# A graph layer and a mixture of experts on one core: a tile's work as stages at fixed chunk offsets, two first-layer blocks to a bank, nine short steps first

## The chip, the cores and the metric

The kernel runs on one core of a Trainium2 chip. Its time is the device time of one execution in microseconds (us), and the kernel before took 1339.35 us, the median of 11 runs (1335.19 to 1341.65).

The engines are named as in the profile: PE (TensorE, the matmuls), PEld (its loads of weights, which overlap with the matmuls), DVE (VectorE), ACT (ScalarE), POOL (GpSimd) and SP (SyncE). Each engine executes its own instructions in the order in which the program has them, and waits for the others by semaphores. SPq, ACTq and POOLq are the queues from which an engine starts DMA transfers.

## The reference

6250 nodes have 256 features each. The first layer is a graph convolution over 106250 edges, sorted by target. The second routes every node to the best two of eight experts, each of which is a feed-forward net of 256 to 1024 to 256.

```python
deg_isqrt = jnp.maximum(segment_sum(ones, dst), 1.0) ** (-0.5)
x = x + gnn(layernorm(x))        # norm * segment_sum((norm * (h @ W.T + b))[src], dst)
h = layernorm(x)
scores = h @ Wg.T + bg           # 8 experts
top, idx = top_k(scores, 2); p = softmax(top)
out = sum over the two e of p_e * (relu(h @ W1[e].T + b1[e]) @ W2[e].T + b2[e])
x = x + out
```

Everything is float32.

## The kernel before, in words

The nodes are 49 tiles of 128. After an opening stage (degrees, and a table of the scaled inputs in DRAM) the kernel has a **stream** and a **tail**.

**The stream** is a loop over 831 chunks of 128 edges; an iteration is called a slot here. In each slot `gather` has POOL start an indirect DMA that fetches 128 rows of the table (6 chunks ahead, 24 buffers), `mask` has DVE make the 128x128 matrix that says which edge goes to which node, and `add_up` has PE add the chunk to a sum in PSUM (`ps`). Once all chunks of a tile are in, the tile goes through `join` (DVE sums, ACT copies to `whole`), `turn_sum` (PE transposes, ACT copies), `linear` (PE, tile `pt`) and `route`: DVE normalizes, scores and chooses two experts, PE counts places (`pt` again), and `sort` and `send` order the tile's rows by expert and write them to eight queues in DRAM (`fhq`), 8 DMAs on SP.

**A step** of the experts takes up to 256 rows (four short steps at the end: 128) from the fullest queue. `choose` decides on DVE which; `fetch` has SP load the expert's weights and biases `w1` (1.15 MB) and `w2` (1.03 MB) and the rows `xT`. `up` is one of the 8 blocks of the first layer: PE multiplies into a PSUM tile `ph`, ACT applies bias and relu and writes `hid`. `down` is a quarter of the second layer's work for 128 rows (PSUM tile `py`), after the last of which DVE adds the bias (`y`) and SP writes the result to DRAM (`fyq`). A step of 256 rows is 16 such pieces, 8 of `up` and 8 of `down`; a step of 128 is 8 and 4. `next_piece` puts one piece into the program in each slot of the stream, and a second one in every fourth slot while the next step is ready.

PSUM has eight banks of 2 KB per partition. `ph` has two buffers, each a tile of its own of 256 columns.

**The tail** goes on after the last chunk: one piece per slot, the loads of the remaining steps, and the way back. `read_back` has POOL fetch each node's two results from `fyq` by indirect DMAs (98 in all), DVE adds them to the node's row (`xr`), and the rows are stored. The list `DONE` says after which step which tiles may be read back.

The order in which everything stands in each engine's program is written out by hand: `plan_at` puts a call into a slot, and `in_parts` spreads a generator over slots in a row (one part per slot). In the kernel before, `route` and `fetch` are such generators. 56 steps are planned: 49 that follow tiles 3 to 48 (three tiles are followed by two), then 7.

These lines are the ones that the change of PSUM tiles touches:

```python
ph = psp.tile([P, FT], F32, name="ph")
for k in range(2):
    nc.tensor.matmul(ph[:, :n], w1[...], f["xT"][:, :n, k], start=(k == 0), stop=(k == 1))
nc.scalar.activation(f["hid"][:, b, :n], ph[:, :n], AF.Relu, bias=w1[...])
```

Of the kernel before, what the change touches and what calls it, by code (L numbers as in the profile page):

```python
# [28 lines left out]
NE = 8  # L29
# [8 lines left out]
FIRST_STEP = 3  # L38
EXTRA = (42, 44, 46)
FOLLOWS = [t for t in range(FIRST_STEP, NT) for _ in range(1 + (t in EXTRA))]  # L40
USUAL = len(FOLLOWS) + 7
SHORT = 4
# [16 lines left out]
DONE = ((40, 29), (42, 33), (43, 34), (44, 35), (45, 36), (46, 38), (47, 39), (48, 40), (49, 41), (50, 42),  # L59
        (51, 44), (52, 45), (53, 46), (54, 47), (USUAL - 1, NT))  # L60
LATER = 1 << 17

# [39 lines left out]
LATE = [(3 if FINAL[t + 1] - FINAL[t] == 9 else 2) if t < NT - 2 else 0 for t in range(NT)]  # L102
# [30 lines left out]
def in_order(ctx: ExitStack, tc: tile.TileContext, g: Shared):  # L133
# [8 lines left out]
    yq = dram.tile([P + USUAL * FT, D], F32, name="fyq")  # L142
# [208 lines left out]
    for step, t1 in DONE:  # L351
        nc.vector.memset(bounds[:, t0:t1, :], float(P + (step + 1) * FT))
        t0 = t1
# [21 lines left out]
    zero = keep.tile([P, FT * D // P], F32, name="zero")  # L375
    nc.gpsimd.memset(zero, 0.0)  # L376

# [15 lines left out]
    def mask(c):  # L393
        masks[c] = work.tile([P, P], F16, name="mask", bufs=MASKS + 3)
        r = (P - BASE[c] % P) % P
        nc.vector.tensor_scalar(masks[c], g.col_b[:, r:r + P], g.rel[:, c:c + 1], None, op0=OP.is_equal)  # L396
# [53 lines left out]
    def clear_results():  # L450

        for step in range(USUAL - SHORT, USUAL):
            r0 = P + step * FT + P
            nc.sync.dma_start(yq[r0:r0 + FT - P, :], zero[:, :D])

# [7 lines left out]
    whole, turned_sums, turned_inputs = {}, {}, {}  # L465
# [4 lines left out]
    def join(w):  # L470
# [11 lines left out]
        rolled = new  # L482
        for t, p0, p1 in pieces(n0, n1):
            if p0 == 0:
                whole[t] = work.tile([P, D], F32, name="whole")
            nc.scalar.activation(whole[t][p0:p1, :], new[p0:p1, :], AF.Copy)  # L486

    def turn_sum(t):
        pt = psp.tile([P, 2, P], F32, name="pt", bufs=1)
        u = whole.pop(t)  # L490
        for k in range(2):
            nc.tensor.transpose(pt[:, k, :], u[:, k * P:(k + 1) * P], g.ident)
        uT = work.tile([P, 2, P], F32, name="uT")
        nc.scalar.activation(uT, pt, AF.Copy)
        turned_sums[t] = uT
# [8 lines left out]
    def route(t):  # L504

        nonlocal placed, known, sent
        xt = g.xr[:, t, :]
        pl = turned_sums.pop(t)
        nc.vector.scalar_tensor_tensor(xt, pl[:, :D], g.norm[:, t:t + 1], xt, op0=OP.mult, op1=OP.add)  # L509
        score = work.tile([P, NE], F32, name="score")  # L510
        nc.vector.scalar_tensor_tensor(score, pl[:, D:], g.norm[:, t:t + 1], xg[:, t, :], op0=OP.mult, op1=OP.add)
        yield
        st = work.tile([P, 6], F32, name="st")
        nc.vector.bn_stats(st, xt)
        mv = work.tile([P, 2], F32, name="mv")
        nc.vector.bn_aggr(mv, st)
        v = work.tile([P, 1], F32, name="v")
        nc.vector.tensor_scalar(v, mv[:, 1:2], EPS, None, op0=OP.add)
        yield

# [4 lines left out]
        rstd = guess.bitcast(F32)  # L525
        vh = work.tile([P, 1], F32, name="rv")
        nc.vector.tensor_scalar(vh, v, -0.5, None, op0=OP.mult)
        r = work.tile([P, 1], F32, name="rs")
        for i in range(3):
            if i == 1:  # L530
                yield
            nc.vector.tensor_scalar(r, rstd, rstd, vh, op0=OP.mult, op1=OP.mult)
            nc.vector.tensor_scalar(rstd, r, 1.5, rstd, op0=OP.add, op1=OP.mult)
        yield

        nc.vector.scalar_tensor_tensor(score, minus, mv[:, 0:1], score, op0=OP.mult, op1=OP.add)
        sc = work.tile([P, NE], F32, name="sc")
        nc.vector.scalar_tensor_tensor(sc, score, rstd, bgs, op0=OP.mult, op1=OP.add)
        times = work.tile([P, 1], F32, name="times")
        nc.vector.tensor_scalar(times, rstd, UP, None, op0=OP.mult)  # L540

        mx = work.tile([P, NE], F32, name="mx")
        nc.vector.max(mx, sc)
        ix = work.tile([P, NE], U32, name="ix")
        nc.vector.max_index(ix, mx, sc)
        ixf = work.tile([P, 2], F32, name="ixf")
        nc.vector.tensor_copy(ixf, ix[:, 0:2])
        yield
        sel = work.tile([P, 2, NE], F32, name="sel")
        for j in range(2):  # L550
            nc.vector.tensor_scalar(sel[:, j], g.col_f[:, :NE], ixf[:, j:j + 1], None, op0=OP.is_equal)
        if t == NT - 1:
            nc.vector.tensor_scalar(sel, sel, valid, None, op0=OP.mult)
        chose = work.tile([P, 2, NE], BF16, name="chose")
        both, front = chose[:, 0], chose[:, 1]
        nc.vector.tensor_add(both, sel[:, 0], sel[:, 1])

        nc.vector.tensor_scalar(front, g.col_f[:, :NE], ixf[:, 0:1], None, op0=OP.is_gt)
        nc.vector.scalar_tensor_tensor(front, g.col_f[:, :NE], ixf[:, 1:2], front, op0=OP.is_gt, op1=OP.add)
        if t == NT - 1:  # L560
            nc.vector.tensor_scalar(front, front, valid, None, op0=OP.mult)
        ex = work.tile([P, 1], F32, name="ex")
        nc.vector.tensor_sub(ex, mx[:, 1:2], mx[:, 0:1])
        nc.scalar.activation(ex, ex, AF.Exp)
        yield

        for _ in range(LATE[t]):
            yield
        h2 = work.tile([P, D], F32, name="h2", bufs=3)
        nc.vector.tensor_scalar(h2, xt, mv[:, 0:1], times, op0=OP.subtract, op1=OP.mult)  # L570
        h2s[t] = work.tile([P, 2, D], F16, name="h2s", bufs=3)
        nc.scalar.activation(h2s[t][:, 0], h2, AF.Copy)
        yield
        pp = psp.tile([P, 3, NE], F32, name="pt", bufs=1)
        nc.tensor.matmul(pp[:, 0], below, chose[:, 0], start=True, stop=True)
        nc.tensor.matmul(pp[:, 1:3], every, chose, start=True, stop=True)
        nc.vector.tensor_sub(h2s[t][:, 1], h2, h2s[t][:, 0])
        pr = prob[:, t, :]
        nc.vector.tensor_scalar(pr[:, 1:2], ex, 1.0, None, op0=OP.add)
        nc.vector.reciprocal(pr[:, 0:1], pr[:, 1:2])  # L580
        nc.vector.tensor_mul(pr[:, 1:2], ex, pr[:, 0:1])
        col = work.tile([1, 2, NE], I32, name="col")
        nc.vector.tensor_sub(col[:, 0], filled[0:1, :], head[0:1, :])
        columns_of[t] = col
        yield

        totals = work.tile([P, 2, NE], F32, name="totals")
        nc.vector.tensor_copy(totals, pp[:, 1:3])
        place = work.tile([P, NE], F32, name="place")
        nc.vector.tensor_add(place, pp[:, 0], filled)  # L590
        nc.vector.tensor_add(filled, totals[:, 0], filled)
        nc.vector.tensor_max(most, totals[:, 0], most)
        placed += 1
        spot = work.tile([P, NE], F32, name="spot")
        nc.vector.tensor_add(spot, pp[:, 0], totals[:, 1])  # L595
# [863 lines left out]
```

## Time and profile before

| | |
|---|---|
| runs (11) | 1339.35 us median, 1335.19 to 1341.65 |
| the profiled execution: own time, span | 1338.88 us, 1337.1 us |
| PE busy (share of the span) | 1178.9 us (88%) |
| PEld | 899.4 us (67%) |
| DVE | 985.5 us (74%) |
| POOL | 903.5 us (68%) |
| ACT | 402.4 us (30%) |
| first gather, last gather (start) | 82.33 us, 1127.41 us |
| last chunk added up (start) | 1145.43 us |
| last group of second-layer matmuls (start) | 1315.65 us |

The profile is one execution. Its span runs from the first instruction to the last; the execution's own time is 1.8 us longer than the span, and 0.5 us shorter than the median of the runs. Busy times of PE overstate it, since matmuls are pipelined and their ends are modelled. Matmuls in float32 stand twice in the trace for each one in the program: a step's 16 for the first layer are 32 rows.

### The profile page before, as it was taken

The numbers are of one execution on the slowest core, as the hardware profiler recorded it, in microseconds if no ns is written. First come the engines' busy times: TensorE is split into PE (matmuls) and PEld (weight loads), VectorE is DVE, ScalarE is ACT, GpSimd is POOL, SyncE is SP. The second block draws the span as 40 slices with busy tenths as digits, with TensorE's granted clock in tenths as the row PEclk, the third lists the DMA queues.
The fourth block names the chain that finished last, engine by engine and source line by source line (L and its number), as shares of the span: only waits on it lengthen the run. The fifth ranks groups of instructions, "written<-read, shape, count | busy, mean of one in ns | idle before, by whom it ended". The sixth has DMA issues, their size and how long they took to land.

```text
span 1337.1 us, 23956 instructions
## 1 busy us (share of the span) xinstructions
PE 1178.9 (88%) x6224; PEld 899.4 (67%) x6224; DVE 985.5 (74%) x5327; ACT 402.4 (30%) x931; POOL 903.5 (68%) x984
## 2 busy tenths in 40 slices
PE   4529895999899999999999989999999999799984
PEld 4417663776677677776766766777777777678873
DVE  8842658787888888888788887788877775765542
ACT  2622331232323233233332323232232322222221
POOL 2047777777777777777777777777777775347742
PEclk9999777999999999999999998999999999899987
DMA  8343446888687887877778787878878987679882
GB/s 298 112 158 106 121 137 196 266 253 286 211 287 227 287 261 253 286 241 270 250 261 268 245 279 218 274 243 288 286 234 286 296 295 254 235 244 347 305 304 89
DMA packets 158459, 326.16 MB, mean 244 GB/s; under 512 B 26708, under 2 KB 105256, under 8 KB 143976
## 3 DMA queue, kind: packets, MB, share of 16 engines
q1 hardware_dynamic: 110780, 194.17, 41.5%
q0 software_dynamic: 46864, 129.82, 32.3%
q8 instruction: 51, 0.84, 0.3%
q14 instruction: 96, 0.79, 0.2%
q10 hardware_dynamic: 668, 0.55, 0.1%
HBM read 269.01 MB, written 55.42 MB: 243 GB/s over the span
## 4 chain that ended last, share of the span: by engine, by line
PE 56%; DMA 17%; DVE 15%; issue 4%; ACT 3%; SPq 2%; POOL 2%; POOLq 0%; ACTq 0%; DVEq 0%
PE ph L730 22%; PE py L740 16%; PE ps L403 9%; DMA rows<-ftable,src 7%; DMA xT<-fhq 5%; PE pt L501 3%; DMA fhq<-ordered 2%; PE ph L446 2%; SPq L641 2%; DMA yb<-fyq,rowat 2%; DVE mask L396 2%; PE px L629 2%; PE px L435 1%; DVE rolled L481 1%; DVE y L744 1%
## 5 line engine op out<-in xcount | busy, mean ns | idle before, releaser
L389 POOL DMA_INDIRECT rows<-ftable,src x831 | 791.2, 952 | 253.4 <-issue 99.5
L730 PE MATMUL ph<-xT,w 128*128 128x256 f32 (+1 forms) x1792 | 468.3, 390 | 28.8 <-DMA xT<-fhq 19.0
L740 PE MATMUL py<-w,hid 128*128 128x256 f32 x1728 | 436.4, 382 | 4.9 <-DVE y L744 4.9
L730 PEld LDWEIGHTS ph<-xT,w 128*128 128x128 f32 x1792 | 320.9, 191 | 125.5 <-issue 29.2
L740 PEld LDWEIGHTS py<-w,hid 128*128 128x128 f32 x1728 | 330.0, 192 | 84.2 <-issue 6.8
L403 PE MATMUL ps<-rows,mask 128*128 128x512 f16 x831 | 319.4, 398 | 51.5 <-DMA fyq<-zero 29.7
L732 ACT ACTIVATE hid<-ph,w 128x256 f32<-128x256 f32 (+1 forms) x448 | 204.8, 466 | 287.5 <-PE ph L730 276.6
L396 DVE TENSOR_SCALAR mask<-col_b,rel 128x128 f16<-128x128 bf16 x831 | 210.0, 272 | 26.8 <-PE ps L403 26.5
L486 ACT ACTIVATE whole<-rolled 32x256 f32<-32x256 f32 (+2 forms) x156 | 64.5, 414 | 346.5 <-DVE rolled L481 346.0
L800 POOL DMA_INDIRECT yb<-fyq,rowat x98 | 94.4, 963 | 87.3 <-DMA w<-in_W 23.6
L403 PEld LDWEIGHTS <-mask 128*128 128x128 f16 x831 | 86.8, 105 | 76.6 <-POOL keep L462 26.1
L744 DVE TENSOR_TENSOR y<-py,w 128x256 f32<-128x256 f32 x108 | 45.5, 421 | 93.3 <-PE py L740 91.5
L478 DVE SCALAR_TENSOR_TENSOR rolled<-rolled,keep,ps 128x256 f32<-128x256 f32 x149 | 70.6, 474 | 18.9 <-PE ps L403 17.7
L808 DVE SCALAR_TENSOR_TENSOR xr<-yb,prob,xr 128x256 f32<-128x256 f32 x98 | 46.0, 483 | 52.2 <-DMA yb<-fyq,rowat 51.0
L481 DVE TENSOR_TENSOR rolled<-ps,rolled 128x256 f32<-128x256 f32 x150 | 63.6, 424 | 5.2
L501 PE MATMUL pt<-gw,uT 128*128 128x264 f32 x196 | 56.9, 417 | 2.0 <-DVE spot L595 2.0
L509 DVE SCALAR_TENSOR_TENSOR xr<-pt,norm,xr 128x256 f32<-128x256 f32 x49 | 23.7, 483 | 43.1 <-PE pt L501 43.1
L446 PEld LDWEIGHTS ph<-wg,turned 128*128 128x128 f32 x196 | 38.2, 286 | 16.8 <-ACT turned L438 16.0
L501 PEld LDWEIGHTS pt<-gw,uT 128*128 128x128 f32 x196 | 40.0, 206 | 13.7 <-DVE spot L595 2.1
L199 PE MATMUL count<-oh,ol 128*16 128x8 bf16 (+2 forms) x898 | 29.0, 174 | 22.5 <-DVE oh L188 18.2
L376 POOL MEMSET zero<- 128x512 f32 x1 | 0.5, 524 | 64.6 <-DMA ftable<-tab 64.6
L199 PEld LDWEIGHTS <-ol 128*16 128x16 bf16 x898 | 28.7, 109 | 22.8 <-DVE ol L185 16.6
(188 smaller groups left out, 1144.4 us busy)
## 6 DMA issues: line engine op xcount, KB each, us to landing
w<-in_W SPq DMA_DIRECT2D x56, 1152.0 KB
w<-in_W SPq DMA_DIRECT2D x56, 1028.0 KB
fhq<-ordered SPq DMA_DIRECT2D x392, 64.0 KB
fyq<-y SPq DMA_DIRECT2D x108, 128.0 KB
xT<-fhq SPq DMA_DIRECT2D x52, 256.0 KB
rows<-ftable,src POOLq DMA_INDIRECT x831
out<-xr POOLq DMA_DIRECT2D x11, 512.0 KB
xr<-in_x SPq DMA_DIRECT2D x6, 896.0 KB
```

The costliest lines, as they stand in the source:

```text
L389: nc.gpsimd.indirect_dma_start(out=rows[c], out_offset=None, in_=table[:, :], in_offset=bass.IndirectOffsetOnAxis(ap=g.src[:, c:c + 1], ax ...
L396: nc.vector.tensor_scalar(masks[c], g.col_b[:, r:r + P], g.rel[:, c:c + 1], None, op0=OP.is_equal)
L403: nc.tensor.matmul(sums[w], masks.pop(c), rows.pop(c), start=(c == chunks[0]), stop=(c == chunks[-1]))
L446: nc.tensor.matmul(px, xT[:, k, (t - t0) * P:(t - t0 + 1) * P], wg[:, k, :], start=(k == 0), stop=(k == 1))
L478: nc.vector.scalar_tensor_tensor(new, rolled, keeps[kept[w]], ps[:, 0:D], op0=OP.mult, op1=OP.add)
L481: nc.vector.tensor_add(new, ps[:, D:2 * D], new)
L486: nc.scalar.activation(whole[t][p0:p1, :], new[p0:p1, :], AF.Copy)
L501: nc.tensor.matmul(pl, uT[:, k, :], gw[:, k, :], start=(k == 0), stop=(k == 1))
L730: nc.tensor.matmul(ph[:, :n], w1[:, k * H + b * P:k * H + (b + 1) * P], f["xT"][:, :n, k], start=(k == 0), stop=(k == 1))
L732: nc.scalar.activation(f["hid"][:, b, :n], ph[:, :n], AF.Relu, bias=w1[:, 2 * H + b:2 * H + b + 1])
L740: nc.tensor.matmul(f["py"], f["hid"][:, b, a * P:(a + 1) * P], f["w2"][:, b * D:(b + 1) * D], start=(b == 0), stop=(b == HB - 1))
L800: r = nc.gpsimd.indirect_dma_start(out=yb, out_offset=None, in_=yq[0:P + (upto + 1) * FT, :], in_offset=bass.IndirectOffsetOnAxis(ap=where ...
```

## The change

- **Stages.** `route` is cut into 15 functions, listed in `STAGES` with the slot at which each stands, counted from the tile's start `FROM[t]`. Tiles start at least 13 slots apart. `join` moves one slot later, and its ACT copies (`part_of`) two slots after it; `turn_sum` and its ACT copy (`keep_turned`), `sort` and its ACT copy with `send` (`send_rows`) stand in different slots. A tile's rows are sent 24 slots after its start; those of the last tile are sent at slot 860, counted on past the last chunk (before: 847).
- **Steps.** `STREAM` lists the slot at which each of 49 steps is chosen, and its rows: the first nine have 128. `TAIL` has 11 more, five of 256 rows and six of 128. That makes 45 steps of 256 rows and 15 of 128 (before: 52 and 4). The first step is chosen at slot 74 (before: 89).
- **Pieces.** Slots have a budget: 1250 ns less 225 for the chunk and less what the tile's tasks in the slot are put at (`TASKS`). Pieces are put in while the budget is positive.
- **Two blocks to a bank.** `ph` is now a tile of two blocks of 256 columns, a whole bank; even blocks use its first half, odd ones its second. There are still two buffers, now two full banks.
- **Smaller ones.** `y` and its store (`leave`) stand one slot after the last `down`; `w1` and `w2` are loaded only when a step at least three back is through; `mask` has 14 buffers (9 before); `clear_results` and a memset of `zero` on POOL are gone; `DONE` has other pairs.

```diff
-FIRST_STEP = 3
-EXTRA = (42, 44, 46)
-FOLLOWS = [t for t in range(FIRST_STEP, NT) for _ in range(1 + (t in EXTRA))]
-USUAL = len(FOLLOWS) + 7
-SHORT = 4
+STREAM = ((74, 128), (83, 128), (94, 128), (103, 128), (112, 128), (121, 128), (130, 128), (139, 128),
+          (148, 128), (175, 256), (194, 256), (213, 256), (232, 256), (249, 256), (266, 256), (283, 256),
...
+          (839, 256))
+TAIL = (256, 256, 256, 256, 256, 128, 128, 128, 128, 128, 128)
+ROWS_OF = [n for s, n in STREAM] + list(TAIL)
+SLOT = 1250
+CHUNK = 225
+SPARE = 2000
+TASKS = dict(turn_sum=220, linear=890, rank=100, sort=430, inputs_turned=800, inputs_scored=1570)
+PIECES = {FT: (915, 870), P: (600, 870)}
...
+FROM = []
+for t in range(NT):
+    FROM.append(max(FINAL[t] + 1, FROM[-1] + 13 if FROM else 0))
...
-        masks[c] = work.tile([P, P], F16, name="mask", bufs=MASKS + 3)
+        masks[c] = work.tile([P, P], F16, name="mask", bufs=MASKS + 8)
...
+    STAGES = ((9, add_sums), (10, guess_root), (11, better_root, 2), (12, better_root, 1), (12, score_nodes),
+              (13, choose_experts), (14, scale_rows), (16, rank), (PLACED, place_rows), (18, place_sorted),
+              (19, place_queued), (20, mark_slots), (21, weigh), (SORTED, sort), (SENT, send_rows))
...
         if b == 0:
             f["hid"] = work.tile([P, HB, FT], F32, name="hid")
-        ph = psp.tile([P, FT], F32, name="ph")
+        if b % 2 == 0:
+            f["ph"] = psp.tile([P, 2, FT], F32, name="ph")
+        ph = f["ph"][:, b % 2]
         for k in range(2):
             nc.tensor.matmul(ph[:, :n], w1[:, k * H + b * P:k * H + (b + 1) * P], f["xT"][:, :n, k],
                              start=(k == 0), stop=(k == 1))
...
         if i % 4 == 3:
-            y = work.tile([P, D], F32, name="y", bufs=4)
-            nc.vector.tensor_add(y, f["py"], f["w2"][:, HB * D:])
...
+            plan_at(s + 1, leave, step, a, f["py"], f["w2"])
...
-        tasks.setdefault(chunks[-1] + 1, []).insert(0, (join, (w,)))
+        tasks.setdefault(chunks[-1] + 2, []).insert(0, (join, (w,)))
+        plan_at(chunks[-1] + 4, part_of, w)
...
+    for step, (s, n) in enumerate(STREAM):
+        in_parts(s, fetch, step)
+        last = max(t for t in range(NT) if FROM[t] + PLACED < s)
+        earliest[step] = max(s + LEAD[0], FROM[last] + SENT + LEAD[1])
...
-                next_piece(s)
-                if s % 4 == 0 and earliest.get(done + 1, NC) <= s:
+                credit = min(credit + SLOT - CHUNK - busy.get(s, 0), SPARE)
+                while credit > 0 and ready(s):
+                    credit -= PIECES[ROWS_OF[done]][cur >= HB]
                     next_piece(s)
```

## The prediction

> **What bounds the kernel now.** I read the windows by stage first, then the timeline of POOL, the chain, and the timeline around one step's first layer.
>
> ```profile
> 217.00:1102.00 885.00, 834.60 (x3847) 622.39 (x3845) 724.57 (x4128) 274.06 (x640) 670.16 (x704) 0.99 0.81 263
> 1146.00:1180.00 34.00, 23.90 (x94) 18.66 (x93) 28.10 (x173) 6.65 (x16) 14.31 (x16) 0.85 0.79 271
> 1180.00:1279.00 99.00, 99.00 (x450) 84.09 (x449) 58.05 (x243) 26.56 (x56) 70.47 (x75) 1.00 0.89 307
> 1279.00:1320.00 41.00, 35.14 (x194) 29.66 (x192) 13.22 (x51) 11.76 (x32) 14.70 (x16) 0.92 0.65 232
> ```
>
> Columns: stretch, length, busy us of PE, PEld, DVE, ACT, POOL, then PE's granted clock. PE is busy 94% of the stream and all of the middle of the tail.
>
> ```profile
> 1126.15 0.95 POOL L389 DMA_INDIRECT rows<-ftable,src  x1 [0.30 <-PE py L740]
> 1127.41 0.94 POOL L389 DMA_INDIRECT rows<-ftable,src  x1 [0.30 <-issue]
> ```
>
> POOL starts a gather every 1.25 us from 82.33 to 1127.41, never held up: two clocks run side by side, POOL's 1.25 us per slot, and PE's work. PE adds the last chunk at 1145.43, 18 us after its gather started; mid-stream that lag is 7 to 13 us. So PE is just about as slow as POOL. The chain shows what PE costs:
>
> ```profile
> 1180.34 7.21 PE ph L730 x32
> 1187.56 6.91 PE py L740 x32
> ...
> 1251.04 7.26 PE ph L730 x32
> ```
>
> A full step is 7.21 + 6.91 = 14.1 us, a block of the first layer 7.21/8 = 0.90. Per tile (17 slots, 21.25 us) PE has 17 chunks at 0.22 (chain, ps L403) = 3.7, a step 14.1, and 1.65 for transposes, the linear layer, places and sort (chain: pt L492 0.22, pt L501 0.89, px L629 0.44, 0.1): 19.5 us. Spare: 1.75.
>
> Now the first layer from near, in the timeline: a full step, then a short one.
>
> ```profile
> 1250.67 7.20 PEld L730 LDWEIGHTS ph<-xT,w 128*128 128x128 f32 x32
> 1250.88 7.41 PE L730 MATMUL ph<-xT,w 128*128 128x256 f32 x32
> ...
> 1252.03 0.47 ACT L732 ACTIVATE hid<-ph,w 128x256 f32<-128x256 f32 x1 [7.38 <-PE ph L730]
> 1252.89 0.47 ACT L732 ACTIVATE hid<-ph,w 128x256 f32<-128x256 f32 x1 [0.38 <-PE ph L730]
> ```
>
> ```profile
> 1279.15 4.66 PE L730 MATMUL ph<-xT,w 128*128 128x128 f32 x32
> 1279.86 0.77 ACT L732 ACTIVATE hid<-ph,w 128x128 f32<-128x128 f32 x2 [6.94 <-PE ph L730]
> 1280.28 0.98 PEld L730 LDWEIGHTS ph<-xT,w 128*128 128x128 f32 x8 [0.25 <-ACT hid L732]
> 1281.04 0.82 ACT L732 ACTIVATE hid<-ph,w 128x128 f32<-128x128 f32 x2 [0.41 <-PE ph L730]
> ```
>
> ACT evicts block n while PE computes block n+1, in the other buffer: in the full step PE never waits. In the short one it waits 0.2 us per two blocks for an eviction, which makes them 1.18 us apart.
>
> **The change, part by part.**
>
> *The bank (the part that decides).* The order of the changed program, with the semaphores that each instruction waits for, has this in every pair of blocks:
>
> ```
> L767 Matmult ph_20003<-xT_19759,w1_19747 128x128 x2
> L767 Matmult ph_20003<-xT_19759,w1_19747 128x128 [waits Activation_49]
> ```
>
> The value waited for is the one that the eviction of the even block just before it brings. Before, a block waits for the eviction two blocks back. So nothing of PE's runs beside that eviction but what the program puts between: PE stands, and all PE work queued behind it stands too (chunks, `down`, other tiles' matmuls).
>
> The price of one wait, where nothing lies between. The full step's first matmul starts at 1250.88 (0.21 after its load of weights), so the block ends at 1251.78; ACT starts at 1252.03, 0.25 later, and takes 0.47; the next load of weights follows an eviction after 0.05 (1279.86 + 0.37 = 1280.23, then 1280.28), its matmul 0.21 after that: 0.25 + 0.47 + 0.05 + 0.21 = 0.98 us. In the short step: from 1279.15 + 0.49 (eight loads take 0.98, a block has four) = 1279.64 to 1280.28 + 0.21 = 1280.49: 0.85. No row has this very wait, and a wait can't gain; the nearest total is `PEld ph L730 <- ACT hid L732`, 24.7 us in 44 waits, 0.56 each: the low end. High end 1.2, an ACT that is half of another instruction late. I take 0.98 and 0.85, read from the same engines' same instructions.
>
> The Trainium skill ("PSUM — Partial Sum Buffer", PSUM bank collisions raise a hardware error) says that PE's writes and ACT's reads must be kept apart by bank and not by address, since disjoint columns of one bank collide. That speaks against this change: by the rule the sum is the forecast, and by address, with the halves overlapping, it would be the 1326 of the second rival. No run here shows a collision.
>
> How often. The program has 240 such waits. In the stream 152 in full steps: 66 with nothing between, 55 with one chunk (0.22, leaving 0.76), 31 with more (a `down` or a tile's matmuls; 2.7 us left in all): 64.7 + 41.8 + 2.7 = 109 us, 2.87 per step. 36 in short steps, 16 bare, 16 with a chunk, 4 with more: 13.6 + 10.1 + 1 = 25 us. In the tail 28 full: 26.7 us. And 24 short: a pair takes 0.49 + 0.85 + 0.49 = 1.83 for 1.18 before, +2.6 per step.
>
> *The stream.* Per tile PE needs 19.5 + 2.87 = 22.4, and keeps some idle time: before, 885.0 - 834.6 = 50.4 us in 41.6 tiles, 1.2 each, of which rows and `xT` (14.8 and 19.0 us in the list of waits, about 0.8 a tile) are waits that a PE that runs late no longer has. 22.4 + 0.4 to 22.4 + 0.9, say 22.95, against POOL's 21.25: 1.7 us per tile lost, over the 37 tiles from chunk 200 to 830 63 us. Chunks 75 to 200 (nine short steps, 156 us of POOL): by the rows 27 us of chunks, 82 of steps, 12 of tiles, 8 of the last inputs, 25 of waits; and some 14 for a clock that was granted at 0.53 to 0.83 from 140 to 240 us: 168, +12. POOL's 24 buffers are 30 us, so gathers will wait for PE for the first time; SP's loads and DVE's masks wait along. Last chunk: 1127.4 + 11 (lag at chunk 75 by then) + 12 + 63 = 1213, +68 on 1145.4.
>
> *The tail.* From the last chunk to the last `py` before: 1319.3 - 1145.4 = 174 us, of which steps 148 (in the program's order 8 full first layers, 4 short, 83 quarters at 0.864). Now 7 full first layers, 6 short and 88 quarters: 50.5 + 28.0 + 76.0 = 154.5 us, and waits 26.7 + 6 x 2.6 = 42, and the last tiles' own matmuls 4: 200.5. Stalls: before 15.6 where tiles 47 and 48 pass DVE (1146 to 1180, PE 23.9 of 34), 8 among the short steps. Now tile 48's stages stand apart, but the first of the late steps (`choose` at slot 862) needs that tile's rows: eight DMAs 4.7, landing 3.2 to 4.7 (chain, fhq), `xT` 5.2 to 6.7: some 15 us, covered by 12 pieces, 12 us. About 8 in all: 209, +35.
>
> *The end.* Three tiles are read back last, not two: two more indirect DMAs of 1.25 us: +2.5.
>
> *Edits at about nothing.* `mask` buffers (DVE waits 26.5 us for PE there, and isn't late for it), the missing memset (0.5 us before the first gather), the later `join`, `part_of` and `leave`: covered by PE being the bound. Nine short steps ask 2.18 MB of weights every 9 slots, with gathers and the rest some 310 GB/s, where the tail before moves 307: at worst 10 us, in the 12 above or hidden by PE. Steps: 384 rows fewer, 3.5 us less in PE by 14.1 and 8.1, inside the counts above. SP's order loses nothing; it waits less for buffers.
>
> *Sum.* 1337.1 + 68 + 35 + 2.5 = 1443 us span; own time 1.8 more, and the median of the runs stands 0.5 above the profiled execution: 1445 us.
>
> **Rivals.**
>
> *The waits are cheap (0.56), and the stream's slack takes most of them.* Then 79 us in the stream, 1.67 per tile: 19.5 + 1.67 + 0.4 = 21.6, 13 us over POOL; last chunk 1127 + 11 + 17 = 1155; tail 191; end 20: 1366. For it: 55 waits have a chunk beside them, and POOL's clock has 1.75 us to spare. Against: 82 of 188 have nothing.
>
> *The waits cost nothing, and the rest decides: faster.* Without them PE's stream fits into POOL's (19.5 + 1.2 in 21.25), the last chunk is added 7 us after its gather, 1134 (-11); tail 155 + 4 + 8 stalls, and short first layers at 0.98 per pair instead of 1.18, -5: 162 (-12); end +2.5: 1337.1 - 11 - 12 + 2.5 = 1317, with 9 us for the transfers among six short steps in a row 1326. From there the waits may add about 11 us before the sum is slower than before: 0.2 us each in the tail's 52, if the stream hides its own. For that ACT's 0.47 itself would have to vanish.
>
> *PE's clock falls.* Before, the granted clock falls where PE idles: 0.85 from 1146 to 1180, with 10 of 34 us idle. A full pair is now 2.78 us with 0.98 idle, a short one 1.83 with 0.85. If a quarter of the steps run at half clock: +65, 1510. Against: the short steps before, with PE waiting 0.2 of 1.18, kept 1.00 from 1295 on.
>
> **How the numbers follow.** My forecast 0.80, cheap waits 0.09, the falling clock 0.06, faster 0.05. High end of the price (1.2): stream 161 and 33, 107 + 20 over POOL, tail 229: 1514. The range for 8 in 10 cuts the faster case and the tails of the two prices: 1370 to 1500. Within 0.2% is what a measurement here can't tell from no change: 0.01 for it, faster 0.04, slower 0.95.
>
> **What would show it.** Right: a large wait of PEld (or PE) `ph` for ACT `hid`, some 240 times, 150 us and more in sum; a full first layer of 11.1 us in the tail instead of 7.21, a short one of 7.3; gathers that stop coming every 1.25 us and wait for PE `ps`; the last chunk near 1213. Wrong: a first layer of 7.2 us in the tail, a last gather still at 1127, or a first layer at 11 us and yet a last chunk near 1150, which would mean the stream had room that I don't see.

## The result, and the profile after

The changed kernel takes 1390.82 us (median of 8 runs, 1389.86 to 1394.82), the kernel before 1338.69 beside it: a ratio of 1.0394, 95% interval 1.0382 to 1.0406. On the chip of a later run it was 1405.97 beside 1338.07, 1.0487 (1.0451 to 1.0524). It is slower, as forecast, but by 52 to 68 us and not by 106. The profiled execution has a span of 1393.6 us (before: 1337.1). In bank_per_step and bank_per_step_2, further on, two of the four executions were in a slower state with a lower PE clock, and their times are the medians of the other two.

The windows by stage, of the changed kernel (stretch, length, busy us of PE, PEld, DVE, ACT and POOL, then PE's granted clock):

```profile
217.00:1102.00 885.00, 805.72 (x3756) 591.63 (x3756) 691.04 (x3985) 263.79 (x640) 657.01 (x693) 0.99 0.79 255
1135.00:1180.00 45.00, 41.68 (x191) 30.40 (x190) 31.62 (x192) 11.82 (x28) 11.39 (x13) 1.00 0.61 206
1180.00:1279.00 99.00, 82.11 (x345) 63.27 (x344) 60.87 (x310) 21.07 (x47) 55.16 (x59) 0.95 0.82 289
1279.00:1380.00 101.00, 79.59 (x419) 65.05 (x417) 39.80 (x185) 25.20 (x64) 39.45 (x43) 0.99 0.65 225
```

In the same 885 us of the stream PE starts 3756 matmuls where it started 3847, and in the middle of the tail it is idle for 17 of 99 us where it was idle for none. The granted clock stays at 0.95 to 1.00 in these stretches, so this is nearly all waiting and not a slower PE.

One full first layer of the tail, in the timeline (start, us, engine, instruction, count, idle time before and its releaser):

```profile
1243.89 1.06 PE L767 MATMUL ph<-xT,w 128*128 128x256 f32 x4
1245.04 0.47 ACT L769 ACTIVATE hid<-ph,w 128x256 f32<-128x256 f32 x1 [7.38 <-PE ph L767]
1245.57 1.66 PEld L767 LDWEIGHTS ph<-xT,w 128*128 128x128 f32 x8 [1.04 <-ACT hid L769]
1245.57 2.08 PE L767 MATMUL ph<-xT,w 128*128 128x256 f32 x8 [0.61 <-ACT hid L769]
1246.78 0.47 ACT L769 ACTIVATE hid<-ph,w 128x256 f32<-128x256 f32 x1 [1.26 <-PE ph L767]
1247.69 0.47 ACT L769 ACTIVATE hid<-ph,w 128x256 f32<-128x256 f32 x1 [0.43 <-PE ph L767]
1248.21 2.08 PE L767 MATMUL ph<-xT,w 128*128 128x256 f32 x8 [0.56 <-ACT hid L769]
```

The first block runs from 1243.89. ACT evicts it from 1245.04 to 1245.51. Only then, at 1245.57, do the odd block and the even one behind it start, eight matmuls in a row; then PE stands again, until the eviction that starts at 1247.69 is through. A pair takes 1248.21 - 1245.57 = 2.64 us, where two blocks took 1.80. The load of weights and its matmul start at the same moment after such a wait.

The list of waits, with the gathers' line of before as the last one, and the chain:

```profile
PEld ph L767 <- ACT hid L769: 181.0, 211, 1.3
POOL rows L403 <- issue: 141.1, 455, 1.6
PE ph L767 <- ACT hid L769: 96.8, 205, 0.8
POOL rows L403 <- PE ps L417: 73.6, 198, 1.5
POOL rows L389 <- PE ps L403: 64.2, 209, 0.8
```

```profile
1216.54 7.06 DMA xT<-fhq
1223.74 2.06 PE ph L767 x4
...
1237.15 6.91 PE py L777 x32
...
1254.66 6.91 PE py L777 x32
...
1316.68 1.19 PE ph L767 x8
1318.31 1.19 PE ph L767 x8
1320.67 3.45 PE py L777 x16
1330.71 3.45 PE py L777 x16
```

A full step goes from one `py` group to the next in 17.51 us (14.1 before), a short one in 10.04 (8.0 before), with pairs of short blocks 1.63 apart. `py` itself is as long as before, 6.91. The first two rows of the chain are the one long stop of the tail, 6.2 us of PE until the rows `xT` of the first late step land. PE's granted clock is 0.50 from 1224 to 1228, just after it, so that step's first four matmul rows take 2.06 us and not 1.06, and its first layer 13.25 us and not 10.6.

POOL, in its timeline:

```profile
1127.20 0.95 POOL L403 DMA_INDIRECT rows<-ftable,src  x1 [0.30 <-PE ph L767]
1129.10 0.94 POOL L403 DMA_INDIRECT rows<-ftable,src  x1 [0.95 <-PE ps L417]
...
1142.85 0.95 POOL L403 DMA_INDIRECT rows<-ftable,src  x1 [0.30 <-PE ph L767]
```

In the list of waits 0.30 us stands in front of most gathers, whatever they are put down to; what changed is the longest wait for `ps`, 1.5 us for 0.8. Most gathers still start 1.25 us apart, but 36 of them (13 before) start more than 1.4 us after the last, as the one at 1129.10 after 1.90 us, which POOL starts when PE has added a chunk (`ps`) and so freed one of the 24 buffers. By the starts of gathers and chunks, PE runs 4.6 us behind its gather at chunk 75, 20 at chunk 200, and 30 from chunk 600 on. The last gather starts at 1142.85 (before 1127.41), the last chunk is added at 1172.6 (before 1145.4).

By parts: the stream +27.1 us, the tail from the last chunk to the last `py` 201.7 for 173.8 (+27.9), the end 19.3 for 17.8 (+1.5): +56.5 of span.

### The profile page after: what moved, and what is told of

Read it like the earlier page. It is cut to its first block, busy times and chain, and to the rows that moved or that the text cites. A ratio compares the mean times of both kernels' runs of the same rounds, so it can differ in the third digit from the quotient of the medians.

```text
span 1393.6 us, 24212 instructions
## 1 busy us (share of the span) xinstructions
PE 1188.3 (85%) x6304; PEld 889.0 (64%) x6304; DVE 983.2 (71%) x5416; ACT 403.6 (29%) x963; POOL 901.0 (65%) x983
## 4 chain that ended last, share of the span: by engine, by line
PE 67%; ACT 9%; DVE 8%; issue 7%; DMA 7%; SPq 1%; POOL 1%; ACTq 0%; POOLq 0%; DVEq 0%
PE ph L767 29%; PE py L777 20%; PE ps L417 8%; ACT hid L769 6%; PE pt L517 3%; PE ph L460 2%; DMA w<-in_W 2%; DMA rows<-ftable,src 1%; DMA fhq<-ordered 1%; PE px L649 1%; DMA xT<-fhq 1%; DVE mask L410 1%; SPq L672 1%; PE px L449 1%; PE count L216 1%
## 5 line engine op out<-in xcount | busy, mean ns | idle before, releaser
L767 PE MATMUL ph<-xT,w 128*128 128x256 f32 (+1 forms) x1920 | 478.7, 378 | 110.2 <-ACT hid L769 96.8
L767 PEld LDWEIGHTS ph<-xT,w 128*128 128x128 f32 x1920 | 329.2, 193 | 250.7 <-ACT hid L769 181.0
L777 PE MATMUL py<-w,hid 128*128 128x256 f32 x1680 | 413.4, 379 | 0.0
L769 ACT ACTIVATE hid<-ph,w 128x256 f32<-128x256 f32 (+1 forms) x480 | 214.3, 446 | 513.5 <-PE ph L767 442.7
L777 PEld LDWEIGHTS py<-w,hid 128*128 128x128 f32 x1680 | 317.5, 190 | 68.2
L417 PE MATMUL ps<-rows,mask 128*128 128x512 f16 x831 | 310.1, 401 | 40.3 <-DMA rows<-ftable,src 37.6
L410 DVE TENSOR_SCALAR mask<-col_b,rel 128x128 f16<-128x128 bf16 x831 | 203.5, 268 | 8.3 <-PE ps L417 8.2
L524 DVE SCALAR_TENSOR_TENSOR xr<-pt,norm,xr 128x256 f32<-128x256 f32 x49 | 23.7, 483 | 135.1 <-PE pt L517 135.1
L588 ACT ACTIVATE h2s<-h 128x256 f16<-128x256 f32 x49 | 20.3, 415 | 173.7 <-DVE h L579 173.7
L460 PEld LDWEIGHTS ph<-wg,turned 128*128 128x128 f32 x196 | 38.7, 290 | 15.7 <-ACT turned L452 14.1
```

The lines of the kernel that those rows point to most:

```text
L417: nc.tensor.matmul(sums[w], masks.pop(c), rows.pop(c), start=(c == chunks[0]), stop=(c == chunks[-1]))
L460: nc.tensor.matmul(px, xT[:, k, (t - t0) * P:(t - t0 + 1) * P], wg[:, k, :], start=(k == 0), stop=(k == 1))
L767: nc.tensor.matmul(ph[:, :n], w1[:, k * H + b * P:k * H + (b + 1) * P], f["xT"][:, :n, k], start=(k == 0), stop=(k == 1))
L777: nc.tensor.matmul(f["py"], f["hid"][:, b, a * P:(a + 1) * P], f["w2"][:, b * D:(b + 1) * D], start=(b == 0), stop=(b == HB - 1))
```

## The experiments

The chip of own_banks, two_apart, before_shared and bank_per_step, and that of after_3, part_in_chunk, own_part_in_chunk and bank_per_step_2, were slower: the kernel before took 1611 and 1586 us there, 18 to 20% more, and those variants that ran on both kinds of chip 14 to 21% more; names that end in _2 repeat a kernel on another chip. Ratios are to the kernel before of the same chip.

| kernel | us | before | ratio, 95% interval |
|---|---|---|---|
| own_banks | 1604.06 | 1610.77 | 0.9962 (0.9933 to 0.9990) |
| own_banks_2 | 1328.81 | 1338.07 | 0.9934 (0.9916 to 0.9952) |
| two_apart | 1608.11 | 1610.77 | 0.9994 (0.9960 to 1.0027) |
| two_apart_2 | 1327.55 | 1339.49 | 0.9909 (0.9890 to 0.9927) |
| after_2 | 1405.97 | 1338.07 | 1.0487 (1.0451 to 1.0524) |
| own_in_stream | 1354.52 | 1338.07 | 1.0120 (1.0099 to 1.0141) |
| own_in_tail | 1378.18 | 1338.07 | 1.0318 (1.0284 to 1.0353) |
| before_shared | 1676.71 | 1610.77 | 1.0386 (1.0323 to 1.0450) |
| before_shared_2 | 1474.20 | 1339.49 | 1.1004 (1.0986 to 1.1023) |
| after_3 | 1649.61 | 1586.38 | 1.0419 (1.0360 to 1.0477) |
| bank_per_step | 1798.31 | 1610.77 | 1.1164 (with all four 1.1282, 1.1179 to 1.1384) |
| bank_per_step_2 | 1759.30 | 1586.38 | 1.1084 (1.1010 to 1.1158) |
| part_in_chunk | 1665.60 | 1586.38 | 1.0469 (1.0399 to 1.0538) |
| part_in_chunk_2 | 1416.44 | 1341.45 | 1.0551 (1.0522 to 1.0580) |
| own_part_in_chunk | 1594.01 | 1586.38 | 1.0033 (1.0007 to 1.0059) |
| own_no_short | 1325.39 | 1339.49 | 0.9897 (0.9880 to 0.9914) |
| own_last_first | 1326.99 | 1339.49 | 0.9906 (0.9889 to 0.9922) |
| own_best | 1315.69 | 1341.45 | 0.9813 (0.9782 to 0.9844) |

### The sharing alone undone

```diff
-        if b % 2 == 0:
-            f["ph"] = psp.tile([P, 2, FT], F32, name="ph")
-        ph = f["ph"][:, b % 2]
+        f["ph"] = psp.tile([P, FT], F32, name="ph")
+        ph = f["ph"]
```

> The changed kernel with one edit: every first-layer block has a PSUM tile of 128x256 of its own again, in a bank of its own; stages, step sizes and order of all instructions stay. Theory (the 240 waits of odd blocks for the eviction of the block before are the whole loss, and more): the stream loses 2.09 us of stall per tile of nodes, 22.06 - 2.09 = 19.97 us, under the 21.28 us that 17 gathers take, so POOL sets the pace, the last chunk is added near 1135 to 1145 instead of 1172.6, the tail shrinks by the 35 us that its waits took, from 201.7 to about 167, and the end stays at 19: 1320 to 1332 us in all, faster than the kernel before by 0.5 to 1.5%. Rival (the stages, the nine short steps or their order cost time themselves, and the waits only fill time that would be lost anyway): 1355 to 1391 us, slower than the kernel before.

> The same edit as in the run of this name before it (a bank for each first-layer block), once more, because on the chip of that run every kernel was some 20% slower: there the kernel before took 1611 us and PE stood still for 160 us in front of first-layer weight loads for nothing that the profile shows, so that PE was late in every variant and the gathers set the pace in none. Where the kernel before takes about 1339 us: the theory says 1320 to 1332 us, ratio 0.985 to 0.995; the rival (stages or steps cost by themselves) 1355 to 1391. Where it takes about 1610: 0.996 as measured.

The second run takes 1328.8 us, within the theory's range: the rest of the change makes the kernel faster, and two blocks in a bank cost more than the whole loss, 77 us on that chip (after_2 less own_banks_2). On the slow chip of the first run own banks are 0.4% faster than the kernel before. The windows, the chain and the waits of own_banks_2:

```profile
217.00:1102.00 885.00, 820.01 (x3904) 625.59 (x3903) 719.60 (x4147) 273.32 (x661) 669.88 (x706) 0.97 0.84 264
```

```profile
1203.99 6.91 PE py L777 x32
1210.89 7.21 PE ph L767 x32
1218.11 6.91 PE py L777 x32
```

```profile
PEld ph L767 <- ACT hid L769: 9.7, 31, 1.1
POOL rows L403 <- PE ps L417: 52.4, 171, 0.6
```

The full first layer is 7.21 us again and the step 14.1, the wait of 181 us is down to 9.7, PE starts 3904 matmuls in the 885 us where it started 3756, and no wait of a gather for PE exceeds 0.6 us. The last chunk is added at 1133.3, 8 us after its gather started; the tail is 167.7 us.

### Two blocks in a bank, but neighbours in different banks

```diff
-        if b % 2 == 0:
-            f["ph"] = psp.tile([P, 2, FT], F32, name="ph")
-        ph = f["ph"][:, b % 2]
+        if b % 4 < 2:
+            f["ph", b % 2] = psp.tile([P, 2, FT], F32, name="ph")
+        ph = f["ph", b % 2][:, b % 4 // 2]
```

> The changed kernel with one edit: still two blocks in a bank, but the four blocks of two banks take turns (first bank, second bank, first, second), so that a block waits for the eviction of the one two before it and not of the one just before. Both banks are as full as in the changed kernel. Theory (what costs is how soon the waited-for eviction comes): as with a bank for each block, within 5 us of it, no gathers late, 1320 to 1335 us. Rival (two blocks in a bank cost by themselves, whatever the distance): near the changed kernel, 1380 to 1392 us.

> The same edit as in the run of this name before it (two blocks in a bank, but neighbours in different banks), again, beside a kernel before that takes about 1339 us. Theory (the distance to the eviction decides, not that a bank is full): as with a bank for each block, 1329 us, 1325 to 1334. Rival (two blocks in a bank cost by themselves): 1385 to 1406 us as the changed kernel on the chips so far.

The second run takes 1327.6 us, as with a bank for each block. The banks are as full as in the changed kernel; what costs is that the block just before has to be evicted first. The Trainium skill ("PSUM — Partial Sum Buffer", PSUM bank collisions raise a hardware error) wants the accesses of two engines kept apart by bank, and the waits of both programs do so. No run here overlaps them, so none shows a collision.

### The stream alone, the tail alone

```diff
-        if b % 2 == 0:
+        if b % 2 == 0 or step < len(STREAM):
             f["ph"] = psp.tile([P, 2, FT], F32, name="ph")
```

This is own_in_stream, with `b % 2` further on as it was: an even block has a new tile and so has an odd one. own_in_tail has `step >= len(STREAM)`.

> The changed kernel as it is, on the same chip as the next edits. Where the kernel before takes about 1339 us: 1391 us, ratio 1.039. Where it takes about 1610 us, PE is late all through, so that each wait is paid in full: the four waits in eight cost 4/7 of what seven in eight cost there (1817 - 1604 = 213 us), 122 us, and the kernel takes about 1725 us, ratio 1.07.

> The changed kernel with a bank for each block in the 49 steps of the stream only; the 11 steps of the tail and their 28 full and 24 short waits stay. Theory: the part of the stream is gained, that of the tail is not. Where the kernel before takes about 1339 us: last chunk near 1140, tail as in the changed kernel 202, end 19: 1355 to 1368 us. Where it takes about 1610 us: the tail's 35 us above the kernel with a bank for each block, 1640 us. Rival (what is lost in the stream is made good in the tail, since the gathers end later anyway): no gain against the changed kernel.

> The changed kernel with a bank for each block in the 11 steps of the tail only; the waits of the stream stay. Theory: the stream as in the changed kernel, last chunk near 1173, the tail shorter by 35 us, 167, end 19. Where the kernel before takes about 1339 us: 1350 to 1362 us. Where it takes about 1610 us: 35 us below the changed kernel, about 1690 us. The two halves should add up to the gain of the kernel with a bank for each block; if they add to more, the waits of one half hide those of the other.

Own banks in the stream give 51.5 us (1406.0 to 1354.5), in the tail 27.8 (to 1378.2), together 79.2 where both at once give 77.2: the halves add up, and neither makes good for the other. The traces have the parts where they were expected: last chunk at 1134.4 and tail 199.4 in own_in_stream, 1181.3 and 170.6 in own_in_tail. own_in_tail's total lies 16 us above its range because it was laid by the 1391 of the first chip; against the changed kernel on its own chip the gain is 28 for 35 expected.

### More waits

```diff
-        if b % 2 == 0:
+        if b == 0:
             f["ph"] = psp.tile([P, 2, FT], F32, name="ph")
```

> The changed kernel with one edit: all eight blocks of a step use the two halves of one bank in turn and the next step the other bank, so that 7 blocks of 8 wait for the eviction of the block before, where the changed kernel has 4 of 8. Theory: 3 more waits per step at the prices measured in the changed kernel: stream 47 steps x 3 x 0.51 = 72 us, and since the gathers are already held there, all of it is paid; tail 7 full steps x 3 x 0.77 + 6 short x 3 x 0.62 = 27 us: 1391 + 99 = 1490 us, 1465 to 1510. Rival (the loss is not proportional to the number of waits, since the chunks that lie between blocks take up a part of them, or since something else holds PE): under 1440 us.

> The edit of the run of this name before it (7 blocks of 8 wait for the eviction of the block before), again, beside a kernel before of 1339 us. Theory: 3 more waits per step, 47 x 3 x 0.51 = 72 us in the stream and 7 x 3 x 0.75 + 6 x 3 x 0.62 = 27 in the tail, 99 us above the changed kernel, 1485 to 1510 us, ratio 1.11 to 1.13. Rival (not proportional to the number): under 1450 us.

> The changed kernel as it is, so that the next three are read against it on one chip: 1391 to 1406 us beside a kernel before of 1339.

Both of these runs met a slow chip. On that of bank_per_step_2 the kernel with own banks would take 0.9962 x 1586 = 1580 us (the ratio is that of the other slow chip, so this is an estimate), the changed kernel takes 1650 and this one 1759: +70 for four waits in eight, +109 for three more, where 99 were forecast. The loss goes on, and more than in proportion. Why isn't shown: the first waits may find time in which PE would have stood anyway, and PE's clock is lower too (0.88 to 0.89 in these two executions, 0.91 to 0.92 in after_3), which no run here tells apart from the waits.

### The kernel before with shared banks

The edit is the reverse of the first one, in the kernel before.

> The kernel before with one edit, two first-layer blocks in one bank, in the changed kernel's form; its steps and its order stay. Theory: 4 waits in each step at the prices seen in the changed kernel, 0.52 us in the stream's mean, 0.77 full and 0.62 short in the tail. Stream: 20.0 + 2.1 = 22.1 us per tile against 21.28 of the gathers, 0.8 us over some 43 tiles = 35 us, less the 12 us by which PE can still fall behind the gathers before they are held (lag 18 of 30 us): +23. Tail of 8 full and 4 short steps: 32 x 0.77 + 16 x 0.62 = +35. Together 1339 + 58 = 1397 us, 1375 to 1415. Rival (the loss of the changed kernel comes from its stages or steps): under 1355 us.

> The same edit as in the run of this name before it (the kernel before with two first-layer blocks in one bank), again, beside a kernel before that takes about 1339 us. Theory, with the prices seen there: stream 4 waits in each step, nearly all with something between them, 0.5 us each, 2.1 us per tile; 20.0 + 2.1 = 22.1 us against the 21.28 us of 17 gathers, over some 43 tiles 35 us, less 12 us of room in the gather buffers: +23. Tail 32 full waits at 0.75 and 16 short at 0.62: +34. 1339 + 57 = 1396 us, 1375 to 1415, ratio 1.027 to 1.057. Rival (the changed kernel's stages and steps are needed for the loss): under 1355 us.

The second run takes +135 us, far over the +57 of the theory (on the slow chip it is +66). The excess is in the stream: the last chunk is added at 1255.5 us, 110 later than in the kernel before where 23 were expected, and the tail is 25 longer where 34 were. So the four corners on chips of the usual speed are: own banks, the old order 1339; shared, old 1474; own, new 1329; shared, new 1391 to 1406. The new order is worth 10 us with own banks and 68 to 83 with shared ones. The waits and a stretch of the timeline of before_shared_2 show what was missing in the theory:

```profile
ACT whole L486 <- DVE rolled L481: 328.1, 100, 9.7
PEld ph L732 <- ACT hid L734: 228.7, 217, 4.3
POOL rows L389 <- PE ps L403: 151.9, 282, 2.1
```

```profile
612.00 1.06 PE L732 MATMUL ph<-xT,w 128*128 128x256 f32 x4
613.60 0.47 DVE L478 SCALAR_TENSOR_TENSOR rolled<-rolled,keep,ps 128x256 f32<-128x256 f32 x1
614.11 0.42 DVE L481 TENSOR_TENSOR rolled<-ps,rolled 128x256 f32<-128x256 f32 x1
614.56 0.41 ACT L486 ACTIVATE whole<-rolled 32x256 f32<-32x256 f32 x1 [0.43 <-DVE rolled L481]
615.00 0.47 ACT L734 ACTIVATE hid<-ph,w 128x256 f32<-128x256 f32 x1
615.53 1.17 PE L732 MATMUL ph<-xT,w 128*128 128x256 f32 x4 [2.21 <-ACT hid L734]
```

The even block starts at 612.00 and is through by 613.06, but its eviction stands in ACT's program behind the copy to `whole`, which waits for VectorE's sum, which is itself in a line of the tile's scoring work. The eviction starts at 615.00, 2 us late, and PE stands for 2.21 us. The Trainium skill ("PSUM — Partial Sum Buffer", Engine vs sequencer instructions) calls ACT's queue strictly first in, first out, which is what these rows show. I counted, from 300 us to the last chunk, how long an even block's eviction starts after the end that the profile gives its matmuls: 0.41 us in the mean in before_shared_2, with 35 over 0.3 us late that come to 54 us, 23 of them (40 us) right behind `whole`; 0.35 in the kernel before itself, where two banks hide it; 0.05 in the changed kernel. Waits with something between them (a chunk or another piece of PE's work, between the two blocks) cost 0.81 us in the mean here and 0.34 in the changed kernel, at the same median of 0.51. Per tile, from chunk 200 to 830, PE takes 24.0 us, of which some 4.1 are lost to waits in front of `ph`; in the changed kernel it is 22.1, with 2.5.

### One stage put back

```diff
-        tasks.setdefault(chunks[-1] + 2, []).insert(0, (join, (w,)))
-        plan_at(chunks[-1] + 4, part_of, w)
+        tasks.setdefault(chunks[-1] + 1, []).insert(0, (part_of, (w,)))
+        tasks.setdefault(chunks[-1] + 1, []).insert(0, (join, (w,)))
```

This puts the sum and ACT's copy of it to `whole` back into one slot, as before the change; own_part_in_chunk has it in own_banks.

> The changed kernel with one stage put back as it was before: VectorE's sum of a window and ACT's copy of it to `whole` are issued in the same chunk, one chunk after the window's last, where the changed kernel has the sum two chunks after and the copy four. Theory (a wait for an eviction is dear where ACT stands in front of `whole` with the eviction queued behind): ACT's wait for `rolled` rises from 114 us to some 300, the waits with something between them from a mean of 0.34 toward 0.8, 86 x 0.45 = 39 us more in the stream, all of it paid since the gathers are held: 30 to 60 us above the changed kernel on the same chip. Rival (the other stages that were put in other chunks make the difference): less than 10 us above it.

> The edit of the run of this name before it, again. Beside a kernel before of about 1339 us, theory: ACT's wait for `rolled` rises from 114 us to 200 or more, the mean of the waits with something between them from 0.34 to 0.5 to 0.8, and the time to 1410 to 1455 us, 10 to 60 above the changed kernel (1391 to 1406). Rival (the other stages make the difference to the 135 us): at most 1406 us, the mean near 0.34. Beside a kernel before of about 1590 us: 1.047 as measured.

> The same stage put back in the kernel with a bank for each block. Theory: with two blocks of room PE doesn't wait for an eviction that comes 1 to 2 us late, and the gathers set the pace, so it shows in ACT's wait for `rolled` alone: 1326 to 1333 us. Rival (the stages also give time by themselves): 1335 to 1345 us, towards the kernel before.

ACT's wait did what was expected; first the changed kernel, then part_in_chunk_2:

```profile
ACT whole L499 <- DVE rolled L487: 114.4, 39, 6.6
```

```profile
ACT whole L499 <- DVE rolled L487: 261.9, 102, 10.6
```

The time is 10 to 26 us above the changed kernel (1416.4 against 1391 and 1406, other chips), and 16 us above it on the slow chip, where the two intervals overlap. But the mean of the waits with something between them stays at 0.33, as the rival said, and only 5 evictions start over 0.3 us late (35 in before_shared_2). So ACT's longer wait for the sum is not enough: this stage alone doesn't bring back the late evictions. That VectorE's sums come late in before_shared_2 because the tile's whole chain is crowded into few chunks is a guess that fits the rows above; the other stages weren't tried. With own banks the same edit gives 1.0033, on one slow chip, where own banks gave 0.9962 on the other: some 11 us, if the ratio carries over. The theory had expected no change, for a chip on which the gathers set the pace; that case wasn't run.

### The nine short steps

```diff
-STREAM = ((74, 128), (83, 128), (94, 128), (103, 128), (112, 128), (121, 128), (130, 128), (139, 128),
-          (148, 128), (175, 256), ...
+STREAM = ((89, 256), (106, 256), (123, 256), (139, 256), (156, 256),
+          (175, 256), ...
```

With own banks, and each step in `DONE` lower by four.

> A bank for each block, and five steps of 256 rows, started at chunks 89, 106, 123, 139 and 156, in place of the nine of 128 that start at chunks 74 to 148; the rest stays. Theory: with own banks the gathers set the pace from chunk 200 on in either form (PE's chunks run 4 to 10 us behind their gathers, of 30 us of room), and the tail has the same 11 steps, so the nine short steps bring nothing that is seen at the end: last chunk at 1130 to 1137, 1325 to 1333 us. Rival A (the short steps are what brings the last chunk from 1145 to 1133, by starting the experts earlier): last chunk near 1143, 1335 to 1342 us. Rival B (their four extra weight sets and fills of PE cost): 1318 to 1325 us.

It takes 1325.4 us, beside 1327.6 for two_apart_2 and 1327.0 for own_last_first (below) on the same chip. The last chunk is added at 1132.9 and the tail is 167.7 us, as with the nine (1133.3 and 167.7). The nine short steps bring nothing that is seen at the end.

### The end, and a version to keep

```diff
-                if pend and (done == USUAL or len(pend) > 10 or s >= pend[0][0] + 8):
+                if pend and (s + 1 not in tasks or s <= all_sent) and (
+                        done == USUAL or len(pend) > 10 or s >= pend[0][0] + 8):
```

> A bank for each block, and in the tail no adding of read-back rows in a slot just before a result leaves PSUM, so that VectorE takes the last result (y) at once; with own banks it took it 4.0 us after the last matmul's end, behind an addition that waited for its read-back. Nothing else is moved. Theory: the last six read-backs go out 3.5 us sooner, the end after the last second-layer matmul falls from 24.2 to 20 to 21 us: 1325 us, 1323 to 1327. Rival (the end is set by POOL's read-backs and their landing, and VectorE's order doesn't matter): 1328 to 1330 us.

The time, 1327.0 us, can't decide between 1323 to 1327 and 1328 to 1330. The end can: it is 23.7 us (24.2 in own_banks_2), where the theory had 20 to 21. DVE's timeline in own_last_first:

```profile
1302.16 0.42 DVE L789 TENSOR_TENSOR y<-py,w 128x256 f32<-128x256 f32 x1
1305.43 0.48 DVE L867 SCALAR_TENSOR_TENSOR xr<-yb,prob,xr 128x256 f32<-128x256 f32 x1 [2.85 <-DMA yb<-fyq,rowat]
1306.81 0.49 DVE L867 SCALAR_TENSOR_TENSOR xr<-yb,prob,xr 128x256 f32<-128x256 f32 x1 [0.90 <-DMA yb<-fyq,rowat]
1307.21 0.16 DVE L854 SCALAR_TENSOR_TENSOR rowat<-at 128x6 int32<-128x6 f32 x1
```

`y` is taken 0.8 us after the last matmul, but the places of the last read-backs (`rowat`) still stand behind two additions that wait for their rows, so the last six gathers start no sooner. The theory took the wrong instruction of VectorE for the one that counts; that VectorE's order doesn't matter, as the rival had it, isn't shown either.

own_best has this edit too, and the tail without its last two steps (TAIL with four steps of 128 rows; the last pairs of `DONE` are (55, 44), (56, 46) and the last step).

> A bank for each block, the last result taken first by VectorE, and the tail without its last two steps of 128 rows: counted from the routing of these inputs, steps 58 and 59 take no rows (57 takes 22). What is lost is the reserve of two steps before the kernel's slower fallback. The results of nodes are called done at the same steps up to 54, then 44 tiles at step 55, 46 at step 56, the rest at 57. Theory: two short steps are 2 x 8.1 us of PE at the end, 1327 - 16 = 1311 us, 1307 to 1316, ratio 0.976 to 0.982. Rival (the read-backs and stores then end last): 1316 to 1325 us. Beside a kernel before of about 1590 us: 2 x 9 us less than the 0.996 of own banks, 0.985.

It takes 1315.7 us, 0.9813 of the kernel before: the fastest of all. The tail fell by 16.5 us, from 167.7 to 151.2, as the two steps' PE time said; the end grew from 24.2 to 26.3, and the last chunk came 3 us later in this execution. The two steps left out are a reserve against the slower fallback, so this gain holds for inputs routed as these are.

## Why the prediction was right in direction and wrong in size

- **Where it loses, and by which mechanism: right.** The wait of each odd block for the eviction just before it; the gathers held by PE; the waits' place in `ph` for `hid`; the clock staying up. own_banks_2 and two_apart_2 show that it is this wait and nothing else of the change.
- **The failed step: the price of one wait.** The prediction put it at 0.25 + 0.47 + 0.05 + 0.21 = 0.98 us. The first three terms hold: from the end of the even block's matmuls to the odd block's start PE loses 0.76 us in the mean of the 66 bare waits of the stream (those with nothing between the two blocks). The fourth, 0.21 from the load of weights to its matmul, was taken from a running stream and is paid by half: after a wait both start at the same moment (1245.57), and then the first of the odd block's four matmul rows takes 0.33 us to the next one, where it takes 0.23 without a wait. So the tail's bare full wait costs 2.64 - 1.80 = 0.84, and the stream's 0.86. Where something lies between, 0.52 was forecast and PE's stop is 0.34 in the mean of 86 waits; in short steps it is 0.63 bare (forecast 0.85) and 0.36 in the other 20 (0.55). These stops are 97 us in the stream and 35 in the tail; with the slower first rows, 0.1 us in some 210 blocks, 113 and 41 us, where the prediction had 134 and 47. That is 27 us of the 49 by which the span was forecast too long (1443 for 1393.6); the rest is in the terms below.
- **The stream: 1213 forecast, 1172.6 measured.** At chunk 200 the forecast stands at 334.9 + 11 + 12 = 358, the trace has 354.9: the lag at chunk 75 was 4.6 and not 11, the chunks to 200 cost 173 and not 168. From there 855 was forecast and 818 measured, 22.06 us per tile. The waits of odd blocks are 2.44 us of it for 2.87, PE's other idle time 0.34 for some 0.6, PE's work 19.3 for 19.5. A further 5 us are a slip of the sum: POOL was held up now and then before, too ((1127.41 - 82.33) / 830 = 1.259 us per gather, and not 1.25 "never held up"), and the loss against 21.25 us per tile was added to that later end.
- **The tail: 209 forecast, 201.7 measured.** The full first layer takes 10.6 us for 11.1, a short one 6.6 for 7.3, so the waits add 36 us to the layers of before and not 42. The stall before the first late step, put at about 8, was 6.2, and the clock that fell after it cost 2.6 more.
- **The end: +2.5 forecast, +1.5 measured.**
- **Rivals.** Cheap waits (1366) had the price too low, 0.56, and the stream's slack too large, but 1391 lies nearer to it than to 1445. The faster case named what would happen without the waits, 1317 to 1326; own_banks_2 measured that at 1329. The falling clock didn't come from these waits: the granted clock of the changed kernel is 1.00 from 401 to 1220 us, with a stop of 0.3 to 0.8 us in the mean in front of every second block, and falls to 0.50 just after the one stop of 6.2 us, for some 10 us.
- **Not seen by the prediction:** that the price depends on ACT's queue. It took ACT's 0.25 from a tail where ACT has nothing else to do. In the changed kernel that was nearly so in the stream too (0.05 us late in the mean). In the old order the same kind of wait cost 0.81 with something between, and an estimate of before_shared by the changed kernel's prices missed by 78 us the other way.

## What to carry to other kernels

Two PSUM buffers are two only if the block that comes next is in the one that was evicted longest ago; before tiles are packed two to a bank, lay them out so that neighbours in time are in different banks. A wait on another engine costs what stands in that engine's queue, so price it in the stage where it will happen, and price the restart from rows where the engine had actually been waiting. And when one resource sets the pace (here a gather every 1.25 us), the gain of taking waits off another engine ends there: the same reordering was worth 10 us with own banks, where the gathers set the pace, and some 75 with shared ones, where PE did.

## What the runs showed of the hardware that was not expected

On two chips the same programs took 14 to 21% longer (the kernel before 18 to 20%). PE's granted clock was 0.88 to 0.92 there in the mean of the profiled executions (0.94 to 0.97 elsewhere), and PE and ACT stood still for nothing that the profile shows. own_banks and own_banks_2 are the same program; own_banks has on the slow chip:

```profile
PEld ph L767 <- issue: 160.3, 98, 9.8
ACT hid L769 <- issue: 126.0, 84, 8.0
PE ph L767 <- issue: 89.7, 57, 4.2
```

and own_banks_2 has 64.6 us in 41 waits for the first of these. The cause wasn't found. In every trace taken on these chips PE's chunks run 24 us or more behind their gathers from chunk 75 to the end, so PE is the bound throughout and gathers set the pace in no variant; own banks gain 0.4% and not 0.7%, and an edit's worth is another. Among the chips of the usual speed the kernel before stayed within 1338 to 1341 us, while the changed one took 1391 and 1406 on two of them; whether its waits are the reason wasn't looked into.
